# Batch 0's first feed-forward front, tile by tile: statistics, root and VectorE butterflies per token tile, affine step of x on ScalarE

## The chip, the cores and the metric

The kernel runs on one NeuronCore of a Trainium2 chip. The metric is the time of one execution on the device in microseconds (us); the median of three runs of the kernel before is 2125.17 us (2123.82 to 2126.85). PE is the matrix engine (TensorE), DVE VectorE, ACT ScalarE, POOL GpSimd, and SP the engine that issues most DMAs.

## What is computed

Four batches of 512 tokens with 512 features pass through two layers. The part that the change touches is the first half of layer 0:

```python
x = x + tanh(g_xattn[0]) * L0_xattn(ctx_512, layernorm(x))   # graph "attention"
x = x + tanh(g_ffn[0])   * L0_ffn(layernorm(x))              # ternary FFN with Hadamard rotations
...
def L0_xattn(h, adj_raw):                 # adj_raw = layernorm(x), 512 x 512 per batch
    sim = (sum over heads of Q K^T) / (sqrt(32) * 4)
    threshold = the 153rd largest of each row of sim
    A = sigmoid(sim) * (sim >= threshold)
    A = (A + A^T) * 0.5
    return (1 - gamma) * adj_raw + gamma * A
def h_bitlinear(x, w):
    xq = act_quant(fwht(x))               # Walsh-Hadamard transform, 8 bits per token
    return xq @ weight_quant(w).T         # ternary weights
def L0_ffn(x):
    return h_bitlinear(silu(h_bitlinear(x, w_gate)) * h_bitlinear(x, w_up), w_down)
```

Since adj_raw is a layer norm of x itself, the first residual is an affine map of each row of x (its "affine step") plus a multiple of A + A^T. Layer 1 is a latent attention over the context with 16 heads, then a second ternary FFN.

## The kernel before

A batch is four tiles of 128 tokens by 512 features. A token tile of x lives in one buffer, `xs[b, j]`, from its load to the end. Work is written as Python generators; the tile framework then fixes an order of instructions per engine from the order in which they were written, from priorities and from a model of durations. On the chip each engine runs its own list strictly in order and waits on semaphores.

The program has three parts. In the first, batch 0 is alone (`alone[0]` is true): `adjacency(0)` (L395), the ternary weights of the first FFN (`feed_weights`, L243), `ahead()` (L616), which prepares products of weights and context for the later attention, and `feed0(0, w0)` (L469). In the second, `attention` (L835) runs over all batches and head pairs, with `adjacency` and `feed0` of batches 1 to 3, and then the second FFN, woven in. The third is the end of the second FFN. The change is in the first part; what it does to batches 1 to 3 is a matter of signs and names.

`adjacency(b)`: for each of four row tiles j, one matmul gives `psim`, ACT scales it to `sim` (L420), and DVE finds the 153rd largest of each row with 20 rounds of MAX8 (L426) and MATCH_REPLACE8 (L428). STT L434 then writes `adj[:, j, :]`. After all four: statistics of the four x tiles and one root for all (`ln_stats`, L437; its root L153 is on ACT), the columns `kr` and `km` (L440 to L443), and per tile j: four PE transposes of column block j into `padj` (L449), the affine step of x on DVE (L450), `sym = adj + padj` (L454) and `x += c_new * sym` (L455). The statistics and the affine step of batch 0 depend on the loaded x alone, and the framework's order has them early, among the first rounds of MAX8.

`feed0(b)`: the statistics of all four updated tiles and one root (L471), then per tile the normalised tile n (L478), four butterfly instructions of 128x256 on POOL (L481; n to h and back to n), four transposes (`pn`, L484), a copy (`hT_`, L486), four matmuls with a 128x128 Hadamard matrix (`pza`, L490), the absolute maximum (L492), scales, rounding (L499, L501) and transposes (`ptq`, L191) to the quantised `zq`. `tiles` (L302) then weaves two generators: `gated` (L284: `pg` and `pu`, 8-bit matmuls at L291, Silu L296, product L297) and `back` (L507: eight butterflies of 128x1024 on DVE, L513; Hadamard matmuls L519 to L525; maximum L364; rounding L369 and L197; `pd`, L386; x updated, L531).

PSUM is in three pools: `mm` with 4 banks (tags of `mm_ps`), `tr` with 2, `bg` with 2. While batch 0 is alone, `pg` and `pu` come from `mm` (`gate_ps`, L75). So do `ahead`'s products `pO` (L643) and `pk` (L663), the latter copied by ACT (`krs`, L665) and written to DRAM by a DMA that POOL issues (`krd`, L667), with three SBUF buffers between. `padj` comes from `bg`.

Batch 0's order of writing (L898 to L905) is: the rest of the adjacency, then `feed0`, with one step of `ahead` after each step of it.

Of the kernel before, what the change touches and what calls it, by code (L numbers as in the profile page):

```python
# [9 lines left out]
F32 = mybir.dt.float32  # L10
# [5 lines left out]
P = 128  # L16
# [17 lines left out]
def flamingo_kernel(  # L34
# [136 lines left out]
    def ln_tile(dst, src, j, mv, r):  # L171
        nc.vector.tensor_scalar(
            dst, src, mv[:, j, 0:1], r[:, j : j + 1], ALU.subtract, ALU.mult
        )
# [220 lines left out]
    def adjacency(b):  # L395
        cT = front_t(f"cT_{b}")
        nc.sync.dma_start(cT, cxT[:, b * S : (b + 1) * S])
        proj = []
        for i in range(2):
            pq = bg_ps(f"pq_{b}_{i}")  # L400
            nc.tensor.matmul(pq, wqk[:, i, :], cT, start=True, stop=True)
            t = bp.tile([P, S], F32, tag=f"qk{i}", name=f"qk{i}_{b}")
            nc.scalar.copy(t, pq)
            proj.append(t)
        qT, kT = proj
        if alone[0]:
            adj = hp.tile([P, NT, S], F32, tag="hT", name=f"adj_{b}", bufs=1)
        else:
            adj = big(f"adj_{b}").rearrange("p (j s) -> p j s", j=NT)
        for j in range(NT):  # L410
            if j == (0 if alone[0] else NT - 1):
                for k in range(NT):
                    t = xp.tile([P, D], F32, tag="x", name=f"x{b}_{k}")
                    nc.sync.dma_start(t, x[(b * NT + k) * P : (b * NT + k + 1) * P, :])
                    xs[b, k] = t
            i = f"{b}_{j}"
            psim = bg_ps(f"psim_{i}")
            nc.tensor.matmul(psim, qT[:, j * P : (j + 1) * P], kT, start=True, stop=True)
            sim = gate_t(f"sim_{i}")
            nc.scalar.activation(sim, psim, AF.Copy, scale=SIM_SCALE)  # L420
            work = back_t(f"work_{i}")
            cur = sim
            rounds = (TOPK + 7) // 8
            for r in range(rounds):
                m8 = small.tile([P, 8], F32, tag="m8", name=f"m8_{i}_{r}")
                nc.vector.max(m8, cur)  # L426
                if r < rounds - 1:
                    nc.vector.match_replace(work, m8, cur, GONE)  # L428
                    cur = work
                yield 1.45  # L430
            at = (TOPK - 1) % 8
            sg = front_t(f"sig_{i}")
            nc.scalar.activation(sg, sim, AF.Sigmoid)
            nc.vector.scalar_tensor_tensor(  # L434
                adj[:, j, :], sim, m8[:, at : at + 1], sg, ALU.is_ge, ALU.mult
            )
        mv, r = ln_stats([xs[b, j] for j in range(NT)], f"a{b}")  # L437

        kr = small.tile([P, NT], F32, tag="ckr", name=f"ckr_{b}")
        nc.vector.tensor_scalar(kr, r, c_keep, None, ALU.mult)  # L440
        km = small.tile([P, NT], F32, tag="ckm", name=f"ckm_{b}")
        nc.vector.tensor_tensor(km, kr, mv[:, :, 0], ALU.mult)
        nc.vector.tensor_scalar(kr, kr, 1.0, None, ALU.add)  # L443
        yield 5.0
        for j in range(NT):
            i = f"{b}_{j}"
            pt = psb.tile([P, 4, P], F32, tag="bg", name=f"padj_{i}")
            for k in range(NT):
                nc.tensor.transpose(pt[:, k, :], adj[:, k, j * P : (j + 1) * P], ident)  # L449
            nc.vector.tensor_scalar(  # L450
                xs[b, j], xs[b, j], kr[:, j : j + 1], km[:, j : j + 1], ALU.mult, ALU.subtract
            )
            sym = front_t(f"sym_{i}")
            nc.vector.tensor_tensor(sym, adj[:, j, :], pt.rearrange("p k q -> p (k q)"), ALU.add)  # L454
            nc.vector.scalar_tensor_tensor(  # L455
                xs[b, j], sym, c_new, xs[b, j], ALU.mult, ALU.add
            )
            yield 2.0
# [9 lines left out]

    def feed0(b, w):  # L469
        wa, wd, s_gate, s_up, gd = w  # L470
        mv, r = ln_stats([xs[b, j] for j in range(NT)], f"f{b}")  # L471
        yield 4.5
        ready = []
        for j in range(NT):
            u = f"f{b}_{j}"
            n = front_t(f"n_{u}")
            h = front_t(f"h_{u}")
            ln_tile(n, xs[b, j], j, mv, r)  # L478
            for src, dst, g in ((n, h, 2), (h, n, 1)):
                for args in butterfly(src, dst, "p (g t q) -> p g t q", {"g": g}):  # L480
                    nc.gpsimd.tensor_tensor(*args)  # L481
            pt = bg_tr(f"pn_{u}")
            for c in range(NC):
                nc.tensor.transpose(pt[:, c, :], n[:, c * P : (c + 1) * P], ident)  # L484
            hT_ = front_t(f"hT_{u}")
            nc.scalar.copy(hT_, pt.rearrange("p c q -> p (c q)"))  # L486
            pz = bg_ps(f"pza_{u}")
            for c in range(NC):
                cols = slice(c * P, (c + 1) * P)
                nc.tensor.matmul(pz[:, cols], hT_[:, cols], had_sb, start=True, stop=True)  # L490
            amax = small.tile([P, 1], F32, tag="amax", name=f"amaxa_{u}")
            nc.vector.tensor_reduce(amax, pz, AX.X, ALU.max, apply_absolute_value=True)  # L492
            yield 1.2
            m, sc = scales(amax, 1.0 / math.sqrt(D), f"a{u}")
            dg = small.tile([P, 1], F32, tag="dg", name=f"dg_{u}", bufs=6)
            nc.vector.tensor_scalar(dg, m, 1.0 / 127.0, s_gate, ALU.mult, ALU.mult)
            du = small.tile([P, 1], F32, tag="du", name=f"du_{u}", bufs=6)
            nc.vector.tensor_scalar(du, m, 1.0 / 127.0, s_up, ALU.mult, ALU.mult)
            nc.vector.tensor_scalar(h, pz, sc, MAGIC, ALU.mult, ALU.add)  # L499
            q = bp.tile([P, D], BF, tag="qa", name=f"qa_{u}")  # L500
            unmagic(q, h)  # L501
            zq = bp.tile([P, NC, P], BF, tag="zq", name=f"zq_{u}", bufs=4)
            turned(q, zq, 1, f"a{u}")
            ready.append((zq, dg, du))
            yield 2.0

        def back(j, ya, du):  # L507
            u = f"f{b}_{j}"
            yb = big(f"yb_{u}")

            for src, dst, g in ((ya, yb, 8), (yb, ya, 4), (ya, yb, 2), (yb, ya, 1)):
                for args in butterfly(src, dst, "p (g t q) -> p g t q", {"g": g}):
                    nc.vector.tensor_tensor(*args)  # L513
                    yield 1.3
            for k in range(4):
                pt = bg_tr(f"ph_{u}_{k}")
                for c in range(4):
                    at = (4 * k + c) * P
                    nc.tensor.transpose(pt[:, c, :], ya[:, at : at + P], ident)  # L519
                hT_ = back_t(f"yT_{u}_{k}")  # L520
                nc.scalar.copy(hT_, pt.rearrange("p c q -> p (c q)"))
                pz = bg_ps(f"pzh_{u}_{k}")
                for c in range(4):
                    cols = slice(c * P, (c + 1) * P)
                    nc.tensor.matmul(pz[:, cols], hT_[:, cols], had_sb, start=True, stop=True)  # L525
                nc.scalar.activation(
                    yb[:, k * 512 : (k + 1) * 512], pz, AF.Copy, scale=1.0 / math.sqrt(FF)
                )
                yield 0.3
            pd, col = yield from projected(u, yb, du, wd, gd, j == NT - 1)  # L530
            nc.vector.scalar_tensor_tensor(xs[b, j], pd, col, xs[b, j], ALU.mult, ALU.add)  # L531
            yield 0.8

        yield from tiles(f"f{b}", ready, wa, back, True)
# [177 lines left out]
    class Pair:  # L712


        def __init__(self, b, g):
            self.b, self.g, self.u = b, g, f"{b}_{g}"
            self.qhs, self.ros, self.pps = [], [], {}

        def head(self, i):
            pq = mm_ps(f"pqh_{self.u}_{i}")  # L720
# [9 lines left out]
        def rope(self, i):  # L730
# [10 lines left out]
            for o in range(2):  # L741
# [7 lines left out]
                    for to, fro in ((slice(0, 64), slice(64, P)), (slice(64, P), slice(0, 64))):  # L749
                        nc.vector.tensor_tensor(rs[to, :], both[o][fro, :], sin_q[to, t, :], ALU.mult)  # L750
                nc.gpsimd.tensor_tensor(ro, ro, rs, ALU.add)  # L751
                self.ros.append(ro)

        def rotated(self):

# [4 lines left out]
            for o in range(3):  # L760
                at = 2 * o * 64
                halves(
                    pr, (wr[:, at : at + 64], wr[:, at + 64 : at + P]),
                    (ros[o], ros[2 + o]) if o < 2 else (ros[4], ros[5]),
                    start=(o == 0), stop=(o == 2),
                )
            self.qr = wp.tile([P, S], F32, tag="qr", name=f"qr_{u}", bufs=1)
# [127 lines left out]
        behind.enter_context(tc.issue_after(ins.ins))  # L895
    with behind:
        step(early, 20)
    drain(a0)  # L898
    nc.scalar.dma_start(cos_q, cosq)
    nc.scalar.dma_start(sin_q, sinq)  # L900
    with tc.issue_after(marks["load"].ins):
        first = begin(0, 0)
    for _ in feed0(0, w0):
        step(early, 1)
    drain(early)  # L905
    hidden_T(0)
# [178 lines left out]
```

## Time and profile before

| what | value | from |
|---|---|---|
| median of three runs | 2125.17 us | times |
| the profiled execution: its time, its span | 2130.4 us, 2128.6 us | times, page |
| mean granted PE clock | 0.975 | times |
| busy: PE, DVE, ACT, POOL | 88%, 76%, 57%, 16% of the span | page, part 1 |
| rounds of MAX8 for batch 0 | from 16.96 to 141.04 us | timeline of DVE |
| first `pg` matmul of batch 0 | 163.31 us | timeline of PE |
| first attention product of scores (L781) | 309.92 us | chain of waits |

Part 2 of the page cuts the span into 40 slices of 53 us. The first six show where batch 0 is alone: PE 1 2 5 9 7 8, DVE 7 9 8 7 6 7. From the seventh on, PE is at 9 nearly everywhere. Idle time in the first part is thus idle time of the whole chip; time won there reaches the end only if the start of the attention moves. Spans on POOL are rough, and ends of matmuls are modelled.

### The profile page before, as it was taken

To read this page: it belongs to the slowest core of one execution; us is meant where nothing else is said; L and a number is where in the kernel's file an instruction comes from. 1 tells how busy PE (TensorE), PEld (TensorE's weight loads), DVE (VectorE), ACT (ScalarE), POOL (GpSimd) and SP (SyncE) were. 2 spreads that over 40 slices of the span, in tenths; PEclk is the share of its full clock that TensorE was granted. 3 is DMA by queue.
4 is the path that set the end of the run, shared out by engine and by line. 5 is a ranking of instruction groups with operands and counts; after the bars stand their busy time and mean duration, and the time that the engine had idled before them with its cause. 6 is when DMAs were issued, how large, how long until landed. Compare 5 with 4: busy or idle time off the path is not lost.

```text
span 2128.6 us, 21689 instructions
## 1 busy us (share of the span) xinstructions
PE 1875.0 (88%) x7274; PEld 878.8 (41%) x7274; DVE 1620.9 (76%) x3203; ACT 1216.8 (57%) x1997; POOL 345.9 (16%) x332
## 2 busy tenths in 40 slices
PE   1259789999999989999989898999879999999898
PEld 0125534444454333444543333445433444444444
DVE  7987679997766999966669999676645756766775
ACT  6836535535555554456545544565599565676644
POOL 3032012113011111321111112210111210111000
PEclk9979989999999999999999999999999999999999
DMA  7452101111100211110012111011367111111000
GB/s 261 148 190 88 45 23 50 44 40 41 33 24 27 81 41 49 40 37 24 32 32 63 59 41 49 24 31 37 124 230 263 46 36 51 54 33 43 12 16 25
DMA packets 62175, 137.66 MB, mean 65 GB/s; under 512 B 7152, under 2 KB 14704, under 8 KB 58992
## 3 DMA queue, kind: packets, MB, share of 16 engines
q1 hardware_dynamic: 56592, 120.35, 18.0%
q0 software_dynamic: 4320, 14.16, 1.8%
q10 hardware_dynamic: 1152, 1.77, 0.2%
q8 instruction: 58, 0.95, 0.2%
q14 instruction: 53, 0.43, 0.1%
HBM read 116.33 MB, written 19.92 MB: 64 GB/s over the span
## 4 chain that ended last, share of the span: by engine, by line
PE 43%; DVE 38%; ACT 12%; issue 3%; DMA 2%; POOL 2%; SPq 0%; POOLq 0%; ACTq 0%; DVEq 0%
PE po L823 7%; DVE work L428 7%; DVE m L426 7%; PE pc L811 6%; PE pqh L722 4%; DVE nm L789 4%; DVE ro L745 3%; PE pzh_f L525 3%; DVE rs L750 3%; PE pu_g L291 2%; PE pd_g L386 2%; DVE rs L747 2%; PE pr L708 2%; PE pd_f L386 2%; PE pg_g L291 2%
## 5 line engine op out<-in xcount | busy, mean ns | idle before, releaser
L751 POOL TENSOR_TENSOR ro<-ro,rs 128x512 f32<-128x512 f32 x192 | 252.1, 1315 | 1400.9 <-DVE rs L747 962.6
L792 ACT ACTIVATE pp<-pss,nm 128x512 f32<-128x512 f32 x256 | 175.0, 687 | 222.5 <-DVE nm L789 221.8
L722 PE MATMUL pqh<-hT,wq 128*128 128x512 f32 x512 | 240.6, 611 | 6.4 <-ACT pp L792 4.3
L811 PE MATMUL pc<-pT,kv 128*128 128x512 f32 x512 | 240.0, 600 | 6.7 <-ACT pT L804 6.6
L823 PE MATMUL po<-om,cxo 128*128 128x512 f32 x512 | 231.0, 597 | 0.0
L789 DVE TENSOR_REDUCE nm<-pss 128x1 f32<-128x512 f32 x256 | 169.7, 680 | 69.2 <-PE pss L784 68.5
L426 DVE MAX8 m<-work 128x8 f32<-128x512 f32 x304 | 209.5, 689 | 4.5
L737 PE MATMUL pb<-qh,wc 128*128 128x512 f32 x384 | 193.2, 618 | 14.7 <-ACT qh L727 9.3
L795 ACT ACTIVATE pp<-pp,rsm 128x512 f32<-128x512 f32 x256 | 179.4, 723 | 32.2 <-DVE rsm L794 31.9
L428 DVE MATCH_REPLACE8 work<-m,work 128x512 f32<-128x512 f32 x288 | 194.5, 675 | 0.2
L804 ACT COPY pT<-ppt 128x512 f32<-128x512 f32 x256 | 141.8, 588 | 56.0 <-PE ppt L803 55.6
L803 PE MATMUL ppt<-ident,pp 128*128 128x128 f32 x1024 | 152.0, 282 | 11.2 <-ACT pT L804 7.8
L828 DVE SCALAR_TENSOR_TENSOR x<-po,gt,x 128x512 f32<-128x512 f32 x128 | 95.3, 746 | 82.5 <-PE po L823 81.5
L803 PEld LDWEIGHTS ppt<-ident,pp 128*128 128x128 f32 x1024 | 117.8, 143 | 96.3 <-issue 45.5
L722 PEld LDWEIGHTS pqh<-hT,wq 128*128 128x128 f32 x512 | 95.2, 194 | 133.2 <-issue 96.8
L781 PE MATMUL pss<-kr,qr 64*128 64x512 f32 x256 | 144.6, 645 | 5.8 <-ACT pp L792 5.0
L784 PE MATMUL pss<-kr,qr 64*128 64x512 f32 x256 | 145.6, 649 | 3.3 <-DVE x L828 1.8
L745 DVE TENSOR_TENSOR ro<-pb,cos_q 128x512 f32<-128x512 f32 x192 | 130.5, 680 | 14.8 <-PE pb L737 14.0
L823 PEld LDWEIGHTS po<-om,cxo 128*128 128x128 f32 x512 | 94.1, 190 | 114.3 <-issue 96.0
L811 PEld LDWEIGHTS pc<-pT,kv 128*128 128x128 f32 x512 | 90.8, 190 | 98.9 <-issue 85.3
L708 PE MATMUL pr<-ro,wr 128*64 128x512 f32 x192 | 96.5, 610 | 28.6 <-POOL ro L751 23.0
L737 PEld LDWEIGHTS pb<-qh,wc 128*128 128x128 f32 x384 | 66.0, 192 | 94.8 <-issue 37.7
(263 smaller groups left out, 3147.4 us busy)
## 6 DMA issues: line engine op xcount, KB each, us to landing
wq<-in_wqh SPq DMA_DIRECT2D x64, 256.0 KB, 2.6
om<-omd SPq DMA_DIRECT2D x64, 256.0 KB, 2.8
wc<-in_wkcq SPq DMA_DIRECT2D x32, 384.0 KB, 3.1
krd<-krs POOLq DMA_DIRECT2D x32, 256.0 KB, 2.3
kr<-krd SPq DMA_DIRECT2D x32, 256.0 KB, 2.6
sa_w1v<-in_gvT SPq DMA_DIRECT2D x8, 1024.0 KB, 5.6
sb_w1v<-in_gvT SPq DMA_DIRECT2D x8, 1024.0 KB, 5.3
wr<-in_wqr SPq DMA_DIRECT2D x32, 192.0 KB, 2.4
```

What stands on the lines that cost most here:

```text
L426: nc.vector.max(m8, cur)
L428: nc.vector.match_replace(work, m8, cur, GONE)
L722: nc.tensor.matmul(pq, self.wqs[i][:, c, :], hT[self.b][:, c, :], start=(c == 0), stop=(c == NC - 1),)
L737: nc.tensor.matmul(pb, self.wc[:, at : at + P], self.qhs[i if i < 2 else o], start=True, stop=True)
L745: nc.vector.tensor_tensor(ro, both[o], cos_q[:, t, :], ALU.mult)
L751: nc.gpsimd.tensor_tensor(ro, ro, rs, ALU.add)
L789: nc.vector.tensor_reduce(nm, pss[i], AX.X, ALU.max, negate=True)
L792: nc.scalar.activation(pp, pss[i], AF.Exp, bias=nm, accum_out=sm)
L795: nc.scalar.activation(pp, pp, AF.Copy, scale=rs)
L803: nc.tensor.transpose(pt[:, l, :], pp[:, l * P : (l + 1) * P], ident)
L811: nc.tensor.matmul(pc, kv[self.b][:, l, :], self.pT[i][:, l, :], start=(l == 0), stop=(l == NT - 1),)
L823: nc.tensor.matmul(po, self.cxo[i][:, j * P : (j + 1) * P], self.oms[i], start=(i == 0), stop=(i == 1),)
```

## The change

Four things are changed for batch 0, and the order of writing is rearranged around them.

- The affine step of x runs on ACT (`Identity` with a scale column and a bias column) while `alone[0]` holds. `km` is stored negated, so that it can be a bias; the later batches add it where they subtracted it.
- `padj` takes its PSUM bank from `gate_ps`: an `mm` bank for batch 0 (four of them, where there were two `bg` banks), a `bg` bank for the others as before.
- In `feed0` with `quick` set, each tile has its own statistics and root (`ln_stats([xs[b, j]])`), and the four butterflies per tile go to DVE.
- The driver takes the adjacency's last steps and `feed0`'s first steps in turn: add tile j, then two steps of `feed0` for it. `ahead` no longer steps in that stretch; its steps follow later.

`self.ros` becomes a dictionary of the same tiles.

```diff
-        nc.vector.tensor_tensor(km, kr, mv[:, :, 0], ALU.mult)
+        nc.vector.scalar_tensor_tensor(km, mv[:, :, 0], -1.0, kr, ALU.mult, ALU.mult)
...
-            pt = psb.tile([P, 4, P], F32, tag="bg", name=f"padj_{i}")
+            pt = gate_ps(f"padj_{i}").rearrange("p (k q) -> p k q", k=NT)
...
-            nc.vector.tensor_scalar(
-                xs[b, j], xs[b, j], kr[:, j : j + 1], km[:, j : j + 1], ALU.mult, ALU.subtract
-            )
+            if alone[0]:
+                nc.scalar.activation(
+                    xs[b, j], xs[b, j], AF.Identity, bias=km[:, j : j + 1], scale=kr[:, j : j + 1]
+                )
+            else:
+                nc.vector.tensor_scalar(
+                    xs[b, j], xs[b, j], kr[:, j : j + 1], km[:, j : j + 1], ALU.mult, ALU.add
+                )
...
     def feed0(b, w):
-        mv, r = ln_stats([xs[b, j] for j in range(NT)], f"f{b}")
-        yield 4.5
+        quick = alone[0]
+        if not quick:
+            mv, r = ln_stats([xs[b, j] for j in range(NT)], f"f{b}")
+            yield 4.5
...
-            ln_tile(n, xs[b, j], j, mv, r)
+            if quick:
+                mv, r = ln_stats([xs[b, j]], f"f{b}_{j}")
+                ln_tile(n, xs[b, j], 0, mv, r)
+            else:
+                ln_tile(n, xs[b, j], j, mv, r)
...
-                    nc.gpsimd.tensor_tensor(*args)
+                    (nc.vector if quick else nc.gpsimd).tensor_tensor(*args)
...
-    drain(a0)
...
-    for _ in feed0(0, w0):
+    f0 = feed0(0, w0)
+    step(a0, 1)
+    for _ in range(NT):
+        step(a0, 1)
+        step(f0, 2)
+    drain(a0)
+    for _ in f0:
         step(early, 1)
```

## What the change will do to the time: the prediction

> **What bounds the kernel now.** I read part 2 of the page first: only the first six slices have a PE well below 9. Then I took busy time by stage for the time in which batch 0 is alone, then the chain of waits there, then each engine's timeline.
>
> ```profile
> core 0: us, PE busy (x) PEld busy (x) DVE busy (x) ACT busy (x) POOL busy (x), PEclk, DMA share, GB/s
> 141.90:163.30 21.40, 7.39 (x30) 5.28 (x30) 13.12 (x34) 3.42 (x6) 9.26 (x14) 0.50 0.10 37
> 163.30:209.80 46.50, 46.18 (x221) 25.71 (x221) 36.22 (x55) 29.20 (x46) 11.31 (x18) 0.97 0.23 85
> 209.80:221.00 11.20, 11.14 (x81) 8.14 (x80) 3.05 (x3) 8.57 (x16) 2.16 (x4) 1.00 0.23 91
> 221.00:235.00 14.00, 12.33 (x48) 5.33 (x45) 13.93 (x18) 5.14 (x10) 2.84 (x5) 1.00 0.36 117
> ```
>
> The first row is the stretch from the last adjacency row to the first `pg`: no engine is full, so it is a chain. The next two are PE's (46.18 of 46.50 us), the fourth is DVE's (13.93 of 14.00). Before 141.90 DVE runs MAX8 and MATCH_REPLACE8 without a gap. So batch 0's time is DVE to 141.9, a chain of 21.4 us, PE to 221, DVE to 235, and then a chain again. The chain of waits names the 21.4 us:
>
> ```profile
> 141.16 0.76 DVE adj L434
> 141.96 0.49 PE padj L449
> 142.47 1.28 DVE sym L454 x2
> ...
> 151.82 0.56 DVE n_f L172
> 152.45 1.64 POOL h_f L481 x2
> 154.16 0.73 POOL n_f L481
> 154.93 1.39 PE pn_f L484 x4
> 156.34 0.59 ACT hT_f L486
> 156.98 2.09 PE pza_f L490 x8
> ```
>
> Tile 0's n starts at 151.82, 9.9 us after adj, because all four tiles are added and measured first; then POOL's butterflies take 2.5 us. The timeline of DVE shows the affine step:
>
> ```profile
> 21.99 1.62 DVE L450 TENSOR_SCALAR x<-x,ckr,ckm 128x512 f32<-128x512 f32 x1
> 23.53 0.68 DVE L426 MAX8 m<-work 128x8 f32<-128x512 f32 x1
> 24.14 1.03 DVE L450 TENSOR_SCALAR x<-x,ckr,ckm 128x512 f32<-128x512 f32 x1
> 25.09 0.08 DVE L428 MATCH_VALUE_LOAD work<-m,work 128x8 f32 x1
> ...
> 25.75 0.82 DVE L450 TENSOR_SCALAR x<-x,ckr,ckm 128x512 f32<-128x512 f32 x1
> ...
> 27.09 1.45 DVE L450 TENSOR_SCALAR x<-x,ckr,ckm 128x512 f32<-128x512 f32 x1
> ```
>
> The same four instructions of batch 1, at 290 us, take 0.53 to 0.54 us; here POOL works on the context's rotation from 22.07 on.
>
> **What the Trainium skill says.** "SBUF — State Buffer", Who interferes with whom: DVE and GpSimd have one port pair under an exclusive lock, which a `tensor_scalar` in a two-port mode and a `tensor_tensor` with both inputs in SBUF want; the second to come waits for the whole instruction of the first. The trace agrees: each L450 ends about 0.3 us after a POOL instruction, MAX8 keeps its 0.68 us. "GPSIMD Engine Reference", Elementwise: a float32 `tensor_tensor` takes 1.96 times as long on GpSimd. Here POOL's 128x256 takes 0.73 us; DVE's price is not in the trace, and from its 0.69 at 128x512 and 1.22 at 128x1024 I estimate 0.42, issued every 0.33. "ScalarE: Activation LUTs", What ACT_TABLE_LOAD costs: 1.28 us per change of table; the trace has 1.28, but none of the page's further 1.38 us of draining (a load at 167.30 is followed at 168.60). "TensorE: Matmul & The Clock Gate", The HAM clock gate: an idle PE starts at half clock for about 3.4 us. The first row above shows 0.50, and the change leaves it so.
>
> **The change, part by part.** I compared the order of instructions of both built programs and whom each one waits for. After batch 0's part both are the same on every engine but for renamed tiles, so a shift of its end should reach the end of the run whole.
>
> *Stretch 1, MAX8 rounds.* L450 leaves DVE: the next instruction starts 1.54, 0.95, 0.74 and 1.37 us later than each of them, 4.60 in all. The order also moves the small root and column instructions (L154 to L443). Before, those after the first MAX8 cost 0.74 + 0.11 + 0.12 + 0.12 + 0.12 = 1.2 us. Now all stand after the fifth MAX8, from about 23.4 us on, where POOL works until 31 us, and those that want the port pair wait for POOL. Laid against POOL's timeline, five of them wait 0.6, 0.65, 0, 0.8 and 0.7 us, with their own 0.12 each and two or three others 3.3 us. The first MAX8 starts 0.3 us earlier, since it waits for `sim` alone. Sum: 4.60 + 1.2 + 0.3 - 3.3 = 2.8; I take 2.7. From both sides: no such wait gives 5.1; a wait of up to 1.2 us (the longest POOL instruction) at each gives about 1.0.
> ACT gains four affine steps, priced by L566, the same operation and shape: 0.80 us, 3.2 in all. They stand in front of weight work (L223, L236). Cover: ACT waits 3.18 us for DVE at 35.4 and 4.47 at 88.4, both shorter if DVE is earlier. `sim` of tile 2 comes near 76 us on ACT and DVE wants it near 79: covered; uncovered, at most 3.2 us.
>
> *Stretch 2, the chain.* Let 0 be the end of adj. Three blocks of each `padj` now stand before it (four banks), so one transpose each is left, as long as before: sym at 0.5. Then sym 0.68, x 0.75, statistics 0.67 + 0.17, w 0.17; root on ACT and five small instructions with their gaps 1.5 (150.37 to 151.82 before): n at 4.4, where it was at 9.9. n 0.56, h twice 0.75, tile 1's sym 0.6 in between, n twice 0.75: transposes from 6.7. From there to `pg` 8.4 us before (154.93 to 163.31), and 0.5 more for butterflies of tile 1 that stand between the scales: `pg` at 15.6, where it was at 21.4. Win 5.8.
>
> *Stretch 3, PE.* Nine `pk` that filled PE's idle time before adj (128 to 138 us) now stand behind the gates, because `padj` holds the four `mm` banks. Counted in the order up to `ptq_hf` of tile 0, there are 16 `pk` on either side: the nine push others later. But tile 2's and 3's fronts now come in between, and PE waits for them in order. By adding durations along DVE's and PE's lists: PE waits 0.6 for tile 1's rounding, 0.7 for tile 3's n, 0.3 elsewhere, so 46.5 becomes 48.1. DVE has 16 x 0.33 = 5.3 us of butterflies and 3 x 0.9 of roots more; it was busy 36.2 of 46.5, so they fit, and POOL is off the path. ACT has one more pair of table loads (2.6 us) between Silus, hidden since it was busy 29.2 of 46.5. So 5.8 - 1.6 = 4.2 is left, and 0.1 more after `ptq_hf`, where DVE's queue is shorter: 4.3. Bounds: all fronts hidden, 5.8; each of the three tiles delaying PE by another 0.8 us, 2.
>
> *Stretch 4, the serial end.* Five `pk` (0.86 each) and nine `krs` (0.58 each) now stand between the rounding of tile 1 and that of tile 2. Following ACT's list, tile 2's maximum comes 0.45 us later after the rounding than the 13.0 us of before; the copies otherwise lie in ACT's waits for PE. Tile 1's x update (0.66) now stands behind tile 2's rounding L369, which gives 0.5 back. Net 0; bounds +0.5 and -3.
>
> `kr` of the first pair is queued on SP in front of one `wk` and of cT, and now waits about 35 us more for its DRAM copy; what stands behind it is wanted only 25 us later or more. Nothing.
>
> Sum: 2.7 + 4.3 + 0 = 7.0 us. The profiled execution would go from 2130.4 to 2123.4, 0.33%; carried over to the median of the runs shown, 2125.2 - 7.0 = 2118.2 us.
>
> **Rivals.** *Interleaving gives the front back (same).* Tiles wait for each other across PE, ACT and DVE, PE holds gates behind tile 2's transposes, and stretch 3 keeps 1 us. For it: the granted order puts `pn` of tile 2 between gates of tile 0. Against: DVE has 10 us of slack there. 2.7 + 1 = 3.7 less: 2121.5.
> *The port pair costs nothing (faster by more).* The small instructions meet POOL's gaps: 5.1, and the fronts hide whole, 5.8: 10.9 less, 2114.3. Against: POOL is busy in all but 1 us of 22 to 31.
> *The moved copies sit on the chain (slower).* Place: between the roundings of tiles 1 and 2. Price: 9 x 0.58 + 5 x 0.86 = 9.5 us if nothing covers them, each copy also held by three buffers that wait for a DMA of 2.3 us or more. It decides once more than 7.0 of the 9.5 are uncovered; at the full price 2.5 more than before: 2127.7. For it: ACT runs them in order ahead of tile 2's copies. Against: PE and ACT idle in turn in 235 to 275 (29.5 and 21.7 of 40 us).
> That the change doesn't do what it says is excluded by the order: `feed0`'s work does interleave.
>
> **Numbers.** Forecast 0.60 (gain 4.5 to 9), front given back 0.17, more 0.13, slower 0.10. About 0.2%, 4.3 us, is what a measurement can tell from no change. Of the forecast nearly all is beyond it, 0.58 with 0.13 from the larger gain: 0.71. Within: 0.17 + 0.02 + 0.02 from the slower case's lower edge: 0.21. Slower: 0.08. The range leaves out the slower case and the edge of the larger: 2113.5 to 2122.5.
>
> **What would show it.** Adj's end near 139.2; no L450 on DVE before 30 us and stretched L155 to L440 there; tile 0's n 4.4 us after adj; first `pg` 15.6 after; first `ptq_hf` near 63.5 after (before 67.9); tile 2's L364 13.5 after tile 1's L369; L781 near 303. It is wrong if PE is idle over 3 us between `pg` and `ptq_hf`, or if DVE's MAX8 waits for `sim` of tile 2, or if the attention after L781 takes longer than before.

## The result, and the profile after

The changed kernel takes 2123.11 us in the median of 16 runs (2118.53 to 2130.24), the kernel before 2127.19 us in 16 runs beside them (2123.82 to 2131.84). The ratio is 0.9977 with a 95% interval of 0.9969 to 0.9985, that is 4.9 us less (3.2 to 6.6). A second group of runs, told below, has 0.9964 (0.9952 to 0.9977), 7.7 us (4.9 to 10.2). The forecast was 7.0 less. Its 2118.2 us and its range of 2113.5 to 2122.5 stand against the 2125.2 of three runs; against the 2127.19 of sixteen they are 2120.2 and 2115.5 to 2124.5. The direction holds; 7.0 lies in the second interval and just above the first. But of the two halves of the sum one came out too large and the other too small.

Busy time by stage in the changed kernel, cut at its own marks (end of adj, first `pg`, first `ptq_hf`, tile 1's L364, tile 1's rounding), to be laid beside the rows of the prediction:

```profile
core 0: us, PE busy (x) PEld busy (x) DVE busy (x) ACT busy (x) POOL busy (x), PEclk, DMA share, GB/s
141.20:156.50 15.30, 5.59 (x25) 4.31 (x26) 13.39 (x40) 2.30 (x5) 0.00 (x0) 0.50 0.01 2
156.50:204.20 47.70, 47.49 (x223) 25.83 (x222) 42.98 (x83) 31.19 (x50) 8.04 (x14) 0.96 0.26 93
204.20:215.15 10.95, 10.95 (x80) 8.03 (x80) 3.05 (x3) 8.94 (x17) 2.15 (x4) 1.00 0.22 79
215.15:229.00 13.85, 13.85 (x52) 6.31 (x51) 13.85 (x18) 5.61 (x10) 2.79 (x5) 1.00 0.26 100
```

The chain's stretch is 15.3 us where it was 21.4, with DVE busy for 13.39 of it where it was 13.12 of 21.40: the chain now runs on a nearly full DVE. PE's stretch grew from 46.5 to 47.7. The chain of waits of the changed kernel, for the first stretch:

```profile
140.44 0.76 DVE adj L434
141.25 0.49 PE padj L449
141.76 0.70 DVE sym L459
142.49 0.76 DVE x L460
143.27 0.71 DVE st_f L167
...
145.61 0.56 DVE n_f L172
146.19 0.76 DVE h_f L493 x2
146.95 0.60 DVE sym L459
147.55 0.35 DVE n_f L493
...
148.03 1.10 PE pn_f L496 x4
```

Tile 0's n starts 4.4 us after adj (9.9 before), and tile 1's sym stands between the two butterfly stages, as foretold. The surprise is ahead of all this: adj ends at 141.19, only 0.7 us earlier than before, although L450's four instructions are gone from DVE. The timelines of the changed kernel, first DVE, then ACT (start, duration, engine, line; in brackets the wait and what ended it):

```profile
18.09 0.69 DVE L426 MAX8 m<-sim 128x8 f32<-128x512 f32 x1 [0.69 <-ACT sim L420]
...
24.16 0.69 DVE L426 MAX8 m<-work 128x8 f32<-128x512 f32 x1
26.76 0.18 DVE L154 RECIPROCAL r_a<-t_a 128x4 f32<-128x4 f32 x1 [1.90 <-ACT t_a L153]
...
29.82 0.67 DVE L158 TENSOR_TENSOR r_a<-r_a,t_a 128x4 f32<-128x4 f32 x1
```

```profile
19.05 1.91 ACT L223 ACTIVATE ja_w0g<-sa_w0g 128x2048 bf16<-128x2048 f32 x1 [0.99 <-DMA sa_w0g<-in_gateT]
...
23.20 1.91 ACT L223 ACTIVATE ja_w0g<-sa_w0g 128x2048 bf16<-128x2048 f32 x1 [1.63 <-DMA sa_w0g<-in_gateT]
25.02 0.19 ACT L223 ACTIVATION_READ_ACCUMULATOR ja_w0g<-sa_w0g 128x1 f32 x1
25.23 1.28 ACT L153 ACT_TABLE_LOAD   x1
26.52 0.20 ACT L153 ACTIVATE t_a<-w_a 128x4 f32<-128x4 f32 x1
```

In the kernel before, the root L153 ran on ACT ahead of `sim`, and DVE took its result before the first MAX8:

```profile
15.16 0.20 ACT L153 ACTIVATE t_a<-w_a 128x4 f32<-128x4 f32 x1
15.68 0.16 DVE L154 RECIPROCAL r_a<-t_a 128x4 f32<-128x4 f32 x1
16.01 0.60 ACT L420 ACTIVATE sim<-psim 128x512 f32<-128x512 f32 x1 [0.65 <-PE psim L418]
```

Now the order has it behind two of the gate weights' sums (L223), which wait for their DMA, and ACT loads the root's function table only after them. DVE, in order, stands 1.90 us at L154 with all later rounds behind it. It came there at 24.86: the second sum still took 0.35 us, the table load with its gap 1.31, the root 0.20. So the load is the largest part; before, it ran at 13.87, while DVE was still at the statistics. By these lines, as an estimate, the wait would have been 0.3 us without the second sum's 1.63 us for the DMA, and 0.6 us without the load. The load of `sin_q` (768 KB, ACT's queue) moved the other way, from 19.09 to 12.63, among the gate weights; the second weight's sum begins at 23.20 instead of 20.35.

### The profile page after: what moved, and what is told of

It is laid out like the page before. It is cut to its first block, busy times and chain, and to the rows that moved or that the text cites. A ratio compares the mean times of both kernels' runs of the same rounds, so it can differ in the third digit from the quotient of the medians.

```text
span 2116.7 us, 21703 instructions
## 1 busy us (share of the span) xinstructions
PE 1868.6 (88%) x7274; PEld 874.7 (41%) x7274; DVE 1623.5 (77%) x3233; ACT 1220.8 (58%) x2006; POOL 333.4 (16%) x316
## 4 chain that ended last, share of the span: by engine, by line
PE 44%; DVE 39%; ACT 10%; issue 2%; DMA 2%; POOL 2%; ACTq 0%; SPq 0%; POOLq 0%; DVEq 0%
DVE work L428 8%; DVE m L426 8%; PE po L835 7%; PE pc L823 7%; PE pqh L734 4%; DVE nm L801 4%; DVE ro L757 3%; DVE rs L762 3%; PE pzh_f L537 3%; PE pu_g L291 2%; DVE rs L759 2%; PE pd_g L386 2%; PE pr L720 2%; PE pd_f L386 2%; PE pu_f L291 2%
## 5 line engine op out<-in xcount | busy, mean ns | idle before, releaser
L835 PEld LDWEIGHTS po<-om,cxo 128*128 128x128 f32 x512 | 94.0, 190 | 114.4 <-issue 96.4
```

What stands on the lines that cost most here:

```text
L835: nc.tensor.matmul(po, self.cxo[i][:, j * P : (j + 1) * P], self.oms[i], start=(i == 0), stop=(i == 1),)
```

## The experiments

All marks come from the DVE and PE timelines of one profiled execution of each kernel, in us; lines are those of the changed kernel. The second column is a point in time, each of the next four the stretch from the mark before it. "pq" is the first matmul of batch 1's adjacency (L401). "The weave" stands for the driver's new order of writing, which takes a tile's add and its `feed0` steps in turn. The kernel before was run beside every group, with medians of 2127.19 to 2129.54 us, so sizes across groups are taken from the ratios; 0.001 is 2.1 us.

| kernel | first MAX8 | to end of adj | to first pg | to first ptq_hf | to pq | DVE's longest wait in the rounds |
|---|---|---|---|---|---|---|
| before | 16.96 | 124.9 | 21.4 | 46.5 | 64.9 | none |
| changed | 18.09 | 123.1 | 15.3 | 47.7 | 64.2 | 1.90 at L154 |
| after_again | 17.30 | 124.2 | 15.3 | 47.7 | 64.5 | 2.54 at L154 |
| root_first | 17.31 | 121.0 | 15.3 | 47.3 | 64.1 | none |
| root_first_2 | 18.84 | 120.6 | 15.3 | 47.7 | 64.4 | none |
| sin_pool | 19.43 | 120.8 | 15.3 | 47.0 | 65.1 | none |
| root_late1 | 17.81 | 123.6 | 15.3 | 47.1 | 63.9 | 3.21 at tot_w0g |
| rl_gates | 16.99 | 124.0 | 15.3 | 47.7 | 64.3 | 3.6 at tot_w0g |
| b_aff_act | 19.20 | 121.8 | 21.3 | 47.5 | 65.3 | none |
| aff_dve | 17.77 | 124.8 | 15.3 | 47.7 | 64.5 | 1.71 at L154 |
| no_weave | 18.10 | 123.3 | 21.2 | 46.7 | 64.4 | 1.90 at L154 |
| pool_bf | 18.37 | 123.1 | 17.4 | 50.7 | 66.8 | 1.85 at L154 |
| pool_bf_sp | 16.99 | 123.8 | 17.4 | 50.7 | 65.9 | 2.09 at L154 |
| padj_bg | 17.69 | 123.8 | 15.7 | 66.9 | 68.1 | 2.17 at L154 |

**after_again.** The changed kernel, unedited.

> The changed kernel once more, as the yardstick of this group. Theory (the root of the adjacency's statistics waits behind weight work on ACT): DVE stands about 1.9 us at L154 again, first MAX8 to the end of adj takes about 123.1 us (before 124.95), adj's end to the first pg 15.3, and the ratio to before is near 0.9977 (-4.9 us). Rival (the shortfall in the first stretch is only the late landing of gx_raw, 11.33 instead of 9.88 us, in one execution): with an early landing the wait at L154 shrinks below 0.6 us and adj ends near 139.2.

2123.41 us (9 runs) against 2129.35, ratio 0.9964 (0.9952 to 0.9977). gx_raw (the gates' raw values, which ACT's first activation needs) landed at 10.53, earlier than in the first profile (11.33), and yet DVE stood longer at L154, 2.54 us, and adj ended later, at 141.51. The rival, that only the late start was to blame, falls. The two executions already say what holds adj: from the start of L154 to the end of adj it is 114.4 us in one and 114.9 in the other, so adj follows L154 and not the first MAX8.

**root_first.** One step of the adjacency, its statistics and root, written ahead of the two loads.

```diff
+    step(a0, 1)
     nc.scalar.dma_start(cos_q, cosq)
     nc.scalar.dma_start(sin_q, sinq)
...
     f0 = feed0(0, w0)
-    step(a0, 1)
```

> The changed kernel with one step of the adjacency (statistics and root) written ahead of the loads of cos_q and sin_q; this puts the root on ACT ahead of sim and the weight sums again, and the sin_q load behind two weight sums. Theory: the wait at L154 is gone, first MAX8 to adj's end is 124.95 - 4.60 = 120.4 us instead of 123.1, first MAX8 itself 0.3 later; adj ends 2.4 us earlier than in the changed kernel and the total is 2.4 us lower (about -7.3 us against before, 0.9966). Rival (start noise): no difference to the changed kernel, 123.1 us and 0.9977.

2118.70 us (6 runs), ratio 0.9950 (0.9933 to 0.9967). The wait is gone, and the rounds take 121.0 us (120.4 expected). adj ended at 138.30, 3.2 us earlier than in after_again.

> root_first once more, to narrow its interval (0.9933 to 0.9967). Theory: first MAX8 to adj's end 121.0 us again, no wait at L154, and a ratio to before of 0.995 to 0.9965. Rival (its first result was chance): 0.997 or more, like the changed kernel.

The repetition has 2120.88 us (10 runs), ratio 0.9966 (0.9952 to 0.9980), and 120.6 us in the rounds. The mechanism is confirmed in the profile twice. That the total is below the changed kernel's is not shown: by the ratios root_first is 3.0 to 5.7 us below it, the repetition between 2.3 below and 0.4 above, and the intervals overlap. The repetition also shows what the early root costs. Its DVE timeline:

```profile
17.65 1.07 DVE L155 TENSOR_TENSOR t_a<-r_a 128x4 f32<-128x4 f32 x1
18.76 0.16 DVE L156 TENSOR_TENSOR t_a<-t_a,w_a 128x4 f32<-128x4 f32 x1
18.84 0.69 DVE L426 MAX8 m<-sim 128x8 f32<-128x512 f32 x1
```

L154 to L156 now stand on DVE ahead of the first MAX8. The last x tile landed late here (its L167 began at 15.66, in root_first at 14.49), and L155 took 1.07 us beside POOL (0.47 in root_first), so the first MAX8 came 1.5 us later than in root_first; `sim` was ready at 17.51. Both orders hang the rounds on a transfer, one on x and the other on the weights.

**sin_pool.** The root early, the `sin_q` load early as well.

```diff
-    nc.scalar.dma_start(sin_q, sinq)
+    nc.gpsimd.dma_start(sin_q, sinq)
```

> The changed kernel with sin_q loaded by POOL's queue, early, instead of ACT's. The order then has the root on ACT ahead of sim, as in root_first, while the 768 KB of sin_q still compete with the gate weights. Theory (it is the root's place behind the weight sums that costs, not the competing load): first MAX8 to adj's end 121 us as in root_first (120.99), no wait at L154, total about 4 us below the changed kernel. Rival (the early sin_q load, which makes the gate weights land late, is the cause): DVE waits at L226 or L230 instead, 123 to 124 us, total as the changed kernel.

2122.00 us (16 runs), ratio 0.9973 (0.9966 to 0.9980). The rounds take 120.8 us with no wait: the theory's part about the root holds. The total does not follow, since the first MAX8 came at 19.43: POOL issued the load at 4.37, gx_raw landed at 12.00, and the last L167 began at 16.60, the latest of all kernels here; behind it L135 took 1.09 us on DVE. That the early load pushed these landings back fits, but one execution does not prove it.

**root_late1.** The root ordered 40 us later, behind tile 1's `sim`.

```diff
-        return mv, rsqrt_cols(mv[:, :, 1], k, name)
+        with late or ExitStack():
+            return mv, rsqrt_cols(mv[:, :, 1], k, name)
...
-        mv, r = ln_stats([xs[b, j] for j in range(NT)], f"a{b}")
+        late = lambda: tc.issue_after(sims[1].ins) if alone[0] else ExitStack()
+        mv, r = ln_stats([xs[b, j] for j in range(NT)], f"a{b}", late())
```

> The changed kernel with the root of the adjacency's statistics (L153 to L158) ordered behind sim of tile 1, that is some 40 us later, away from the first weight sums, from POOL's rotation and from the landing of x; all else keeps its order. Theory (the place of the root and its small instructions is what the first stretch gave back): no wait at L154, first MAX8 6.8 us after gx_raw lands whenever x lands, first MAX8 to adj's end 120.5 us (123.1 to 124.2), total about 3 us below the changed kernel, ratio to before near 0.995. Rival (the root waits behind other weight work on ACT wherever it stands): DVE stands over 1 us at L154 again near 63 us, total as the changed kernel.

2122.57 us (22 runs), ratio 0.9969 (0.9960 to 0.9977): no better than the changed kernel. Both the theory and its rival missed. L154 to L158 ran near 60 us without a wait, 0.14 to 0.17 us each. But the DVE timeline has a new stop:

```profile
27.70 0.68 DVE L429 MATCH_REPLACE8 work<-m,work 128x512 f32<-128x512 f32 x1
31.59 0.16 DVE L227 TENSOR_REDUCE tot_w0g<-acc_w0g 128x1 f32<-128x4 f32 x1 [3.21 <-ACT ja_w0g L224]
31.66 0.69 DVE L427 MAX8 m<-work 128x8 f32<-128x512 f32 x1
```

This is the sum over the gate weights (L226 in the changed kernel), which the order keeps in the eighth round. In the changed kernel DVE, held up at L154, came there at 31.81, when ACT had just finished the fourth weight sum (31.10); without the hold it is there at 28.4 and waits for the same DMA. root_first has L226 two rounds later, at 31.99, with the fourth sum done at 29.69. So the cause is not the root alone: two instructions on DVE stand ahead of an arrival that they need, and curing the first exposes the second.

**rl_gates.** root_late1 with tanh and sigmoid of the gates behind the first round of tile 0.

```diff
+        if k == 1:
+            gates()
```

> root_late1 with tanh and sigmoid of the gates (L128, L131) written behind the first round of tile 0, so that ACT copies qk before it waits for gx_raw. Theory: PE waited 4.3 us for these copies; sim no longer sets the first MAX8, but the statistics of x and c_keep on DVE stand right behind, about 2.1 us after the last st_a begins; so the first MAX8 comes 1 us earlier than at the same landings, total 1 us below root_late1. Rival (nothing stands behind): first MAX8 4 us earlier and the total with it.

2122.55 us (22 runs), ratio 0.9975 (0.9966 to 0.9983). The first MAX8 came at 16.99, 0.8 us earlier than in root_late1, with `sim` ready at 13.5; the rival falls. Of the 1 us expected in total nothing came, since DVE then stood 3.6 us at the weights' sum instead of 3.21. An earlier start in front of a fixed arrival is worth nothing.

**b_aff_act.** The kernel before with only the affine step of batch 0 on ACT (and km negated).

```diff
-            nc.vector.tensor_scalar(
+            nc.scalar.activation(xs[b, j], xs[b, j], AF.Identity, bias=km[:, j : j + 1], scale=kr[:, j : j + 1]) if alone[0] else nc.vector.tensor_scalar(
```

> The kernel before with only the affine step of batch 0 on ACT. Theory: L450's 4.60 us leave DVE and nothing takes their place, since the root stays early: first MAX8 to adj's end 120.4 us, adj's end to the first pg unchanged at 21.4, total -4.6 us (0.9978). Rival (the affine steps on ACT push the weight sums, and DVE or the gates wait for them instead): less than 2 us of gain.

2126.92 us (22 runs), ratio 0.9989 (0.9982 to 0.9996): 2.3 us less (0.9 to 3.8), half of what the theory said; the interval leaves the theory's 4.6 out, but not the rival's less than 2. The rounds are 3.1 us shorter instead of 4.6; one of the small instructions, L443, met POOL and took 1.11 us in place of 0.15, and DVE waited 0.26 us for tile 2's `sim`. In the profiled execution x landed 2.0 us later than in the profile of before, which by itself delays the first MAX8 there; what the missing part of the total is, is not settled.

**aff_dve.** The changed kernel with the affine step back on DVE.

```diff
-            if alone[0]:
-                nc.scalar.activation(
-                    xs[b, j], xs[b, j], AF.Identity, bias=km[:, j : j + 1], scale=kr[:, j : j + 1]
-                )
-            else:
-                nc.vector.tensor_scalar(
+            nc.vector.tensor_scalar(
```

> The changed kernel with the affine step of batch 0 back on DVE, where its order has it behind the ninth MAX8 (33 us), after POOL's rotation of the context. Theory (L450's price in the kernel before was its place beside POOL, not its engine): the four cost 0.5 to 0.6 us each, first MAX8 to adj's end 123.1 + 2.2 = 125.3 us, total 2.2 us above the changed kernel (ratio about 0.9987). Rival (the affine step costs 4.6 us wherever it is on DVE): 127.7 us, 0.9999.

2124.58 us (19 runs), ratio 0.9977 (0.9969 to 0.9985), 1.2 us above after_again in the median and 2.8 by the ratios (2.2 expected). The DVE timeline of aff_dve:

```profile
33.74 0.53 DVE L450 TENSOR_SCALAR x<-x,ckr,ckm 128x512 f32<-128x512 f32 x1
...
34.85 0.54 DVE L450 TENSOR_SCALAR x<-x,ckr,ckm 128x512 f32<-128x512 f32 x1
```

Each takes 0.53 to 0.54 us where it took 0.82 to 1.62 beside POOL. From the start of each to the start of the next instruction it is 1.79 us for the four, where the forecast counted 4.60 in the same way: some 2.8 of the 4.60 were the price of the place beside POOL, 1.8 that of the engine. DVE's queue loses less still. From L232, which comes right ahead of the four, to tile 0's adj it is 18.64 us, against 17.27 to 17.29 in the six executions that have the same order without them (changed, after_again, no_weave, pool_bf, pool_bf_sp, padj_bg), so they cost 1.36. The rival's 4.6 falls.

**no_weave.** The adjacency written out in full ahead of `feed0`; per-tile statistics, DVE butterflies and `padj`'s banks kept.

```diff
-    step(a0, 1)
-    for _ in range(NT):
-        step(a0, 1)
-        step(f0, 2)
     drain(a0)
+    f0 = feed0(0, w0)
```

> The changed kernel with the adjacency written out in full before feed0, as in the kernel before; statistics and roots per tile, butterflies on DVE and padj's four banks are kept. Theory (the order of writing brings the gain of the chain): all four sym and x come first, n of tile 0 near 10.3 us after adj (4.42 in the changed kernel), first pg near 21 (15.3), pg to ptq_hf back to 46.5, total about 5 us above the changed kernel. Rival (banks and per-tile roots bring it): first pg under 18 after adj.

2126.26 us (13 runs), ratio 0.9993 (0.9984 to 1.0002). n of tile 0 came 11.1 us after adj, the first `pg` 21.2 after, and PE's stretch fell back to 46.7: the theory's marks within 0.9 us; the total is 3.4 to 6.2 us above the changed kernel by the ratios, where 5 were expected. Without the order of writing, nothing is left that the measurement can tell from the kernel before.

**pool_bf.** The butterflies back on POOL.

```diff
-                    (nc.vector if quick else nc.gpsimd).tensor_tensor(*args)
+                    nc.gpsimd.tensor_tensor(*args)
```

> The changed kernel with the twelve to sixteen butterflies of the first front back on POOL. Theory: POOL takes 3.1 us from n to pn where DVE takes 2.4 with tile 1's sym in between, so first pg 16.0 us after adj (15.3); pg to ptq_hf 47 (47.7), since DVE is emptier; total within 0.8 us of the changed kernel. Rival (DVE's butterflies carry the gain): first pg at 17 or later, total over 2 us above the changed kernel.

2131.63 us (11 runs), ratio 1.0023 (1.0013 to 1.0033): slower than before by 4.9 us, and 10 to 13 above the changed kernel; up to pq the marks show 7.4 to 7.7 of it. The theory's 0.8 was wrong. The first `pg` came at 17.4 and PE's stretch took 50.7. PE's waits from 160 to 260 us in pool_bf (waited for: total, times, longest):

```profile
PE ptq_hf L191 <- ACT q_f L197: 3.0, 2, 2.8
PE ptq_hf L191 <- ACT zT_f L192: 2.0, 2, 1.8
PE pn_f L496 <- POOL n_f L493: 1.8, 3, 1.4
PE pg_f L291 <- ACT sg_f L296: 1.1, 1, 1.1
```

The changed kernel has only the first of the four there, and 1.5 us at pzh. Between `pg` and `ptq_hf` PE was idle 3.18 us of 50.68, where the changed kernel has 0.21 of 47.71, with the same 47.50 busy: that is the whole 3.0, and the waits for n (1.8) and for Silu's sg (1.1) are nearly all of it. With the fronts woven into the gates, PE holds gates behind each tile's transposes, and a front that is late by a POOL stage stops it.

**pool_bf_sp.** pool_bf with the copies of pk sent by SP's queue.

```diff
-                nc.gpsimd.dma_start(d, k)
+                nc.sync.dma_start(d, k)
```

> pool_bf with the copies of pk to DRAM (krd, L679) issued by SP's queue in place of POOL's; the order on PE, DVE and ACT is that of pool_bf. Theory (POOL, in order, holds the krd issues behind the butterflies of tiles 2 and 3, which wait for DVE; so krs buffers come free late, and ACT and PE stand): the first pg stays at 17.4 us after adj, pg to ptq_hf falls from 50.7 to about 47.5, and the total from 8 us above the changed kernel to 3 us or less above it. Rival (POOL's butterflies are themselves too slow for the tiles behind): 50 to 51 us and 8 us as before.

2128.82 us (14 runs), ratio 1.0006 (0.9993 to 1.0018). PE's stretch stayed at 50.7 us to the hundredth, so POOL's queue of DMAs was not what stretched it: the theory falls and the rival holds for that stretch. The part after `ptq_hf` came 0.9 us shorter, which is where the wait for zT had been; the queue is worth about that by the marks. The total is 3.6 us lower by the ratios, with intervals that overlap.

**padj_bg.** `padj` in two `bg` banks as before.

```diff
-            pt = gate_ps(f"padj_{i}").rearrange("p (k q) -> p k q", k=NT)
+            pt = psb.tile([P, 4, P], F32, tag="bg", name=f"padj_{i}")
```

> The changed kernel with padj in the two bg banks as before. Tile 0's chain keeps its length (first pg 15.0 to 15.3 us after adj), but the transposes of tiles 1 to 3 now stand among pza and gates on PE and wait for bg banks. Theory (the four banks are needed for tiles 1 to 3 to come in time): pg to ptq_hf 50 us or more (47.7), total 2 us or more above the changed kernel. Rival (the banks bring nothing; they only push pk behind the gates): pg to ptq_hf 46.5 to 47.7, total equal or lower.

2147.95 us (4 runs), ratio 1.0101 (1.0088 to 1.0115), 26 to 29 us above the changed kernel; in the direction of the theory, whose least size was 2. PE's stretch took 66.9 us. DVE's timeline in padj_bg, the additions of tiles 1, 2 and 3:

```profile
152.63 0.69 DVE L459 TENSOR_TENSOR sym<-adj,padj 128x512 f32<-128x512 f32 x1 [0.16 <-PE padj L449]
...
168.91 0.69 DVE L459 TENSOR_TENSOR sym<-adj,padj 128x512 f32<-128x512 f32 x1 [1.16 <-PE padj L449]
...
189.44 0.69 DVE L459 TENSOR_TENSOR sym<-adj,padj 128x512 f32<-128x512 f32 x1 [0.16 <-PE padj L449]
```

In the changed kernel the last of them is at 163.77. With two banks the transposes of tile 3 stand behind tile 2's whole front on PE, and PE waits for these fronts in order. It is idle 8.1 of the 66.9 us (0.2 of 47.7 in the changed kernel). The rest of the growth, 11 us, is busy time: more `pk` and gate matmuls now stand ahead of `ptq_hf`, and the granted clock is 0.91 instead of 0.96. So the weave needs the four banks, which the forecast had treated as a shift of pk.

## Why the prediction was right, and where its sum was not

*Stretch 1 (2.7 less, bounds 1.0 to 5.1).* Measured from first MAX8 to the end of adj: 1.8 less in one execution, 0.7 in the other, and 0.3 more for the earlier `sim` at equal landings, so 1.0 to 2.2. The term that failed is "those that want the port pair wait for POOL", put at five waits of 0.6, 0.65, 0, 0.8 and 0.7 us, with the rest 3.3 in all (these figures add up to 3.6, which would have left 2.5 and not 2.8). In the changed kernel the five (L155 to L158, L440) took 0.29, 0.15, 0.16, 0.67 and 0.21 us, 1.5 together, about 0.7 more than with no wait at all (0.14 to 0.16 each, L440 0.21, in root_late1 near 60 us); in after_again it is 1.1 more. In place of the rest stands a wait that the working never named: L154 behind the root, behind its table load and two weight sums, behind their DMA, 1.90 and 2.54 us. The sum had counted where the moved instructions stand on DVE and not where L153 stands on ACT. aff_dve adds that most of L450's 4.60 us were the price of a place: at another place on DVE they are 1.79.

*Stretch 2 (21.4 to 15.6).* 15.3 in every kernel that has the weave, DVE's butterflies and the four banks. n at 4.4 was met to 0.02 us; the estimate of 0.42 us for a 128x256 butterfly on DVE was met (0.41 to 0.42 measured, a pair in 0.76). The forecast's own figures put the transposes at 7.1, not 6.7; they came at 6.83. From there to `pg` it took 8.45 us (8.38 before), so the 0.5 for tile 1's butterflies did not come.

*Stretch 3 (+1.6, then -0.1).* 47.7 against 46.5, +1.2; no wait of PE over 3 us between `pg` and `ptq_hf`. The size is near, but not for the reason given, so this is luck. The forecast added three waits of PE (0.6, 0.7 and 0.3 us). The rows of the stretch show PE idle 0.21 us of 47.70, against 0.32 of 46.50 before; what grew is its busy time, 47.49 against 46.18. In root_first and sin_pool PE is idle 0.58 us there, still no 1.6. Most of the growth is the clock. The first 4 us from `pg`, columns as above, first of the kernel before, then of the changed kernel:

```profile
163.31:165.31 2.00, 2.00 (x8) 1.34 (x8) 0.00 (x0) 0.58 (x1) 0.00 (x0) 0.50 0.00 0
165.31:167.31 2.00, 2.00 (x15) 1.52 (x14) 1.03 (x4) 0.59 (x2) 0.57 (x1) 0.90 0.00 0
```

```profile
156.48:158.48 2.00, 2.00 (x8) 1.34 (x8) 1.18 (x4) 1.45 (x3) 0.00 (x0) 0.50 0.00 0
158.48:160.48 2.00, 2.00 (x9) 1.32 (x9) 0.80 (x3) 0.99 (x2) 0.00 (x0) 0.54 0.00 0
```

At half clock PE worked some 2.4 us before and 3.8 after (4.2 in after_again). As an estimate from these rows, that costs 0.7 to 0.9 of the 1.2 us. Why the full clock came later is not shown. The sentence "POOL is off the path" was right of the kernel as changed, but the forecast gave DVE's butterflies no share beyond the first tile's, and pool_bf shows 7.4 to 7.7 us for them up to pq. The weave pays only while each front arrives in time.

*Stretch 4 (0).* From `ptq_hf` to pq 64.9 before, 64.2 and 64.5 after: the moved pk and krs are covered. Tile 2's L364 came 13.06 us after tile 1's rounding, before 13.05 (13.5 foretold).

From the end of adj to pq the gain is 132.8 - 127.2 = 5.7 us and 5.4 in after_again, where the forecast had 4.3; the first stretch gives 1.0 to 2.2 where it had 2.7. The two errors have opposite signs, and 6.4 to 7.9 stands beside 7.0; that the sum came so near is luck too.

*The rivals.* "Interleaving gives the front back" fell by the marks: 1.2 of 6.1 is given back. Its 3.7 us less lies in the first interval of the total, not in the second. "The port pair costs nothing" had its first half nearly right, and the stall took its gain. "The moved copies sit on the chain" fell with stretch 4; the 29.5 and 21.7 us given there are PE's and ACT's busy times, and idle were 10.5 and 18.3 of the 40. What none of them foresaw is that the weave without either of its two companions is slower than no weave: 1.0023 without DVE's butterflies, 1.0101 without the banks, 0.9993 with both and no weave, 0.9977 and 0.9964 with all.

The spans of the two profiled executions differ by 11.9 us, more than the change is worth: 6.4 of it stand at pq, 2.5 come from PE's clock (last section), so that L781 began at 301.05 instead of 309.92, and the rest lies within what runs of one kernel differ by (11.7 us between the lowest and the highest of the changed one). From L781 to the end it took 1818.7 us before, 1815.7 and 1818.2 after, so the attention did not get longer.

root_first has the lowest medians of all kernels that ran, in both of its groups; that it is faster than the changed kernel is not shown, since the intervals overlap.

## What to carry to other kernels

When instructions move, follow each of them on every engine that it touches, up to the transfer it hangs on: the wait that ate this gain stood on ACT behind a table load and a DMA, several steps from the edit. An instruction in an in-order queue that needs a late arrival sets the start of all behind it, and taking it away can merely show the next one that needs the same arrival, as in root_late1; move the arrival, or move all of them. And parts of a pipelining change are not additive: test each with the others in place.

## What was not expected of the hardware

PE's clock fell to half for 7 us in some executions and not in others of the same stretch, where batch 0's hidden transposes leave PE partly idle. Busy time by stage around the `pqh` matmuls, columns as in the first table of this kind, first of the kernel before, then of the changed kernel:

```profile
275.00:285.00 10.00, 7.34 (x23) 2.81 (x22) 7.70 (x24) 8.52 (x13) 0.00 (x0) 1.00 0.00 0
285.00:292.00 7.00, 6.33 (x14) 2.97 (x12) 7.00 (x23) 1.28 (x3) 0.00 (x0) 0.51 0.00 0
```

```profile
268.00:279.00 11.00, 8.34 (x29) 3.54 (x28) 8.14 (x25) 8.64 (x14) 0.00 (x0) 1.00 0.00 0
279.00:287.00 8.00, 7.32 (x20) 3.34 (x19) 8.00 (x23) 1.65 (x3) 0.00 (x0) 1.00 0.11 33
```

The granted clock is 0.51 in the one and 1.00 in the other, the sixteen `pqh` take 9.63 and 7.13 us, and the attention starts 2.5 us later or earlier. In seven of the fourteen profiled executions they take 7.13 us, in the others 8.73 to 9.63. root_first and root_first_2 are the same kernel and have 9.51 and 7.13, so it goes with the execution and not with the edit. The Trainium skill, "TensorE: Matmul & The Clock Gate", What's actually happening, says that activity is judged in a free-running window of about 3.4 us, and that the clock is halved after an idle one. The low clock of some 7 us is about two such windows long. But in the 10 us ahead of it, in the kernel before, PE was never idle for more than 1.25 us at a time, so the page's condition is not seen here; no run shows the windows, and the cause stays open.

A 128x4 instruction on DVE took up to 1.11 us in these runs (L443 in b_aff_act, from 22.84 to 23.95, beside a POOL instruction from 22.66 to 23.92), and 0.14 to 0.21 with POOL idle. The Trainium skill, "SBUF — State Buffer", Who interferes with whom, says that the second engine waits for the whole instruction of the first; the smallest instructions pay that too, which a sum by size misses.
